# Four loads per pair in place of ten: one transfer for a graph's distances, one for its places and weights

## The chip, the cores and the metric

The kernel runs on one core of a Trainium2 chip. The metric is the device time of one execution in microseconds, the median of several runs. Times of single instructions come from one further execution, recorded by the hardware profiler.

## The reference

The input is 128 graphs of 64 nodes, with features `x` of 128 numbers per node and an adjacency `adj` whose entries serve as distances and as weights. Four layers follow each other, each as `x = layernorm(x + layer(x, adj))`. The first two are continuous-filter layers: every edge's distance is expanded in Gaussians and run through a small network; the result, weighted, multiplies the neighbour's features and is summed.

```python
# layer 0 (20 Gaussians); layer 1 is alike with 64 Gaussians, and adj squared as the weight
f_ij = exp(-0.5 / widths**2 * (d_ij - offsets)**2)
rcut = 0.5 * (cos(d_ij * pi / 5) + 1) * (d_ij < 5)
W = (ssp(f_ij @ fw1 + fb1) @ fw2 + fb2) * rcut       # ssp = softplus - log 2
agg = einsum('bjf,bijf->bif', x @ w_in2f, W)
out = ssp(agg @ ow1 + ob1) @ ow2 + ob2
```

Layers 2 and 3 are graph convolutions with a normalised adjacency.

## The kernel before

Most entries of `adj` are zero, so the kernel gathers the edges of each graph into a row of *slots*: for each slot the distance `d` (float32), the place `j` of the neighbour (bfloat16) and the weight `w` (float32). Two graphs make a pair, each on 64 of the 128 partitions; there are 64 pairs in each of the first two layers, in eight sets of eight pairs. The slots per graph (`GSLOTS`) depend on the set: 948 to 1092 in layer 0, 1140 to 1260 in layer 1. The gathering is done on the chip, set by set, beside the work on earlier sets: POOL scatters rows into DRAM (L1030), SP loads them back (`permuted`, L1052), DVE finds the edges (`nearest`, L1179 and L1182), POOL packs them (`pack`, L1097 to L1128), and SP stores the packed slots to DRAM (`store`, L1106), with one DRAM tensor for each of d, j and w of a set.

For each pair, `later_loads` (L1285) brings the slots back, repeated over partitions. In layer 0, 20 Gaussians fill 20 partitions, so the slots of a graph are cut into three chunks, laid one below the other: chunk 0 on partitions 0 to 19 of the graph's half, chunk 1 on 20 to 39, chunk 2 on 40 to 63. Each is a load of its own, so a pair has six loads of d. In layer 1, 64 Gaussians fill the 64 partitions and a graph's d is one load. j and w are each one load per graph, repeated over all 64 partitions. So a pair has ten loads in layer 0 and six in layer 1. All are issued by SP, except the first pair's d, which ACT issues (L1876).

The main loop (L1916) runs over 128 pairs times three chunks. At chunk 0 of pair n it issues the d loads of pair n+2, at chunk 1 those of j and w (`late`). The buffers: three of d, two each of j and w.

```python
def gaussians(n, step):          # d of pair n+1, at chunks 0 and 1 of pair n
    act(d, d, AF.Square, scale=-1.0, bias=w["off"])   # step 0
    act(d, d, AF.Exp, scale=w["coeff"])               # step 1
```

On ACT, `gaussians` turns d into Gaussians in place. On DVE, `one_hot` (L1762) compares j with the partition's number and multiplies by w, at chunk 0 of pair n. Then, chunk by chunk: PE multiplies by the first filter matrix (`px`, L1774), ACT takes Exp and Ln (`h`), PE multiplies by the second (`pw`, L1788), PE picks the neighbours' features through the one-hot (`pg`, L1800), ACT copies them (`g`), DVE multiplies the two (`m`, L1814) and sums slots (`agg`, L1837, L1841). ACT's instructions are recorded at the helper's line L951. The first matrix `fw1` has three versions, one per chunk, with the 20 rows of weights at that chunk's partitions and zeros elsewhere; so `px` takes all 64 partitions of a graph and only one chunk counts.

Within the main loop the program order of every engine, SP included, is the order in which the code is written (`in_order`, L1987); before it, only that of DVE and POOL is (L1914).

Of the kernel before, what the change touches and what calls it, by code (L numbers as in the profile page):

```python
# [12 lines left out]
F32 = mybir.dt.float32  # L13
AF = mybir.ActivationFunctionType
# [5 lines left out]
P = 128  # L20
A = 64
# [3 lines left out]
NG0 = 20  # L25
# [6 lines left out]
BF16 = mybir.dt.bfloat16  # L32
I32 = mybir.dt.int32
U32 = mybir.dt.uint32
U16 = mybir.dt.uint16
# [30 lines left out]
GSLOTS = tuple(tuple(4 * (a + b) for a, b in zip(*both)) for both in zip(EVEN, ODD))  # L66
CHUNKS = tuple(tuple(n // 3 for n in sizes) for sizes in GSLOTS)
MAX_SLOTS, MAX_CHUNK = max(map(max, GSLOTS)), max(map(max, CHUNKS))
# [533 lines left out]
def sparse_stack(ctx: ExitStack, tc: tile.TileContext, t: dict, out: bass.AP, flag):  # L602
# [11 lines left out]
    nc = tc.nc  # L614
# [9 lines left out]
    NS = NP // 8  # L624

    const = ctx.enter_context(tc.tile_pool(name="sconst", bufs=1))
    dram = ctx.enter_context(tc.tile_pool(name="sscratch", bufs=1, space=DRAM))
    edge = ctx.enter_context(tc.tile_pool(name="sedge", bufs=2))
    ps_n = ctx.enter_context(tc.tile_pool(name="sps_n", bufs=2, space=PSUM))

    def pair_at(n):

        return n // NP, (n + 8 * (n // NP)) % NP
# [87 lines left out]
    first = nc.cur_bb.bb.instructions[-1]  # L721

    def dram_ap(ap, offset, dims):
        return bass.AP(tensor=ap.tensor, offset=ap.offset + offset, ap=dims)
# [38 lines left out]
    neg_off = [const.tile([P, 1], F32, name=f"neg_off{i}") for i in range(2)]  # L763
    coeff0 = const.tile([P, 1], F32, name="coeff0")
    width0 = const.tile([P, 1], F32, name="width0")

    fw1 = const.tile([P, 3, C], F32, name="fw1")
# [2 lines left out]
    nc.vector.memset(width0, 1.0)  # L770
    for b in range(2):
        for k in range(3):
            at = slice(A * b + NG0 * k, A * b + NG0 * (k + 1))
            nc.scalar.dma_start(fw1[at, k, :], t["L0_gnn_fw1"])
        at = slice(A * b, A * b + 3 * NG0)
        for to, name in ((width0, "L0_gnn_widths"), (neg_off[0], "L0_gnn_offsets")):
            nc.scalar.dma_start(to[at, :], dram_ap(t[name], 0, [[0, 3], [1, NG0], [1, 1]]))

# [21 lines left out]
    def wait_steps(n):  # L802
        yield from (None for _ in range(n))
# [73 lines left out]
    with (  # L877
# [31 lines left out]
        to = const.tile([NB, 1], U32, name="graph_to")  # L909
# [30 lines left out]
    def act(out_, in_, func, **kw):  # L940
        nonlocal fence, latest, kind
        now = func == AF.Sin
        if kind is None or now != kind:
            fence = latest
            if not now:
                ctx_ = tc.issue_after(fence.ins) if fence is not None else nullcontext()
                with ctx_:
                    fence = nc.scalar.preload_act_table_set("natural_log_exp_and_others")
            kind = now
        with tc.issue_after(fence.ins) if fence is not None else nullcontext():  # L950
            latest = nc.scalar.activation(out_, in_, func, **kw)  # L951
        return latest
# [41 lines left out]
    def find_rows():  # L994
# [17 lines left out]
    perm_again = [dram.tile([P, A + 1], F32, name=f"perm_again{p}") for p in range(16)]  # L1012
    rows1 = [dram.tile([16 * A, 2, 40], F32, name=f"rows{s}") for s in range(NS)]
    slots = {
        (layer, name): [dram.tile([16, GSLOTS[layer][s]], dt, name=f"{name}{layer}_dram{s}") for s in range(NS)]
        for layer in range(2)
        for name, dt in (("d", F32), ("j", BF16), ("w", F32))
    }
    stored = set()

# [59 lines left out]
    def pack(layer, s, d, j):  # L1080

        caps, bases = CAPS[layer][s], BASES[layer][s]
        even, odds = EVEN[layer][s], ODD[layer][s]

        def packed(name, dt):
            tile_ = cpt.tile([P, max(EVEN[layer])], dt, tag=f"{name}{layer}", name=f"{name}{layer}_{s}")
            return tile_[:, 0:even]  # L1090

        dc, jc = packed("dc", F32), packed("jc", BF16)
        for r in range(8):
            to = slice(bases[r], bases[r] + caps[r])
            engine = nc.vector if layer + s == 0 and r % 2 else nc.gpsimd
            if layer == 0:
                engine.tensor_scalar(dc[:, to], d[:, r, 0 : caps[r]], -CUTOFF, None, ALU.max)  # L1097
            else:
                engine.tensor_copy(dc[:, to], d[:, r, 0 : caps[r]])
            if r % 2:  # L1100
                yield

        def store(name, tile_):
            for h, size in enumerate((even, odds)):
                to = dram_ap(slots[layer, name][s], h * even, [[even + odds, 64], [1, size]])
                nc.sync.dma_start(to, tile_[64 * h : 64 * (h + 1), 0:size])  # L1106

        store("d", dc)
        for r in range(8):
            to = slice(bases[r], bases[r] + caps[r])  # L1110
            nc.gpsimd.tensor_copy(jc[:, to], j[:, r, 0 : caps[r]])
        store("j", jc)
        w = packed("w", F32)
        if layer == 0:
            def sine():
                act(w, dc, AF.Sin, bias=half_pi, scale=PI / (2 * CUTOFF))

            if s == 0:
                sine()
            else:  # L1120
                yield from wait_steps(6)
                sines.append(sine)
                while sines:
                    yield
            yield from wait_steps(PACE if s else 0)
            (nc.gpsimd if s else nc.vector).tensor_tensor(w, w, w, ALU.mult)
        else:
            nc.gpsimd.tensor_tensor(w, dc, dc, ALU.mult)  # L1128
        store("w", w)
        stored.add((layer, s))  # L1130
        yield
# [148 lines left out]
    def loads(n, engine=nc.sync):  # L1280
        yield_, late = later_loads(n, engine)
        late()
        return yield_

    def later_loads(n, engine=nc.sync):  # L1285


        layer, p = pair_at(n)
        s = p // 8
        size = GSLOTS[layer][s]  # L1290
        at = (p % 8) * 2 * size
        assert (layer, s) in stored, "slots are read before they are written"
        d = edge.tile([P, MAX_SLOTS], F32, tag="d", name=f"d_{n}", bufs=3)
        j = edge.tile([P, MAX_SLOTS], BF16, tag="j", name=f"j_{n}")
        w = edge.tile([P, MAX_SLOTS], F32, tag="w", name=f"w_{n}")

        def load(to, name, first, n):

            (engine if name == "d" else nc.sync).dma_start(to, dram_ap(slots[layer, name][s], first, [[0, to.shape[0]], [1, n]]))  # L1299

        third = size // 3
        d = d[:, 0 : size if layer else third]
        for b in range(2):
            rows, first = slice(A * b, A * (b + 1)), at + b * size
            if layer == 1:
                load(d[rows], "d", first, size)
            else:
                for k, end in enumerate((NG0, 2 * NG0, A)):
                    load(d[A * b + NG0 * k : A * b + end], "d", first + k * third, third)

        def late():
            for b in range(2):
                rows, first = slice(A * b, A * (b + 1)), at + b * size
                load(j[rows, 0:size], "j", first, size)
                load(w[rows, 0:size], "w", first, size)

        return (d, j, w), late


    def load_a(s):  # L1320
# [142 lines left out]
    w = layers[0]  # L1463
    g0 = const.tile([P, 1], F32, name="g0")
    nc.vector.memset(g0, 0.0)
    act(g0[0:32], g0[0:32], AF.Square, bias=neg_off[0][0:32])
    act(g0[0:32], g0[0:32], AF.Exp, scale=coeff0[0:32])
    u = ps_n.tile([P, 512], F32, tag="n", name="zero_x")
    nc.tensor.matmul(u[:, 0:1], lhsT=fw1[0:32, 0, :], rhs=g0[0:32], start=True, stop=True)
    h0 = const.tile([P, 1], F32, name="h0")  # L1470
    act(h0, u[:, 0:1], AF.Exp, bias=w["b1"])
    act(h0, h0, AF.Ln, scale=0.5, bias=half)
    u = ps_n.tile([P, 512], F32, tag="n", name="zero_w")
# [442 lines left out]
    for i in range(3 * N + 2):  # L1916
        n, k = divmod(i, 3)
# [20 lines left out]
        if n < N:  # L1938
            layer, p = pair_at(n)
            q = next(q for q, group in enumerate(GROUPS[layer]) if group.start <= p < group.stop)  # L1940
            c = dict(
                id=f"{n}_{k}", n=n, k=k, s=p - GROUPS[layer][q].start, at=(layer, q), w=layers[layer],
                size=CHUNKS[layer][p // 8],
            )
            if k == 0:
                if n + GS < N:
                    ahead(n)
                if n + 2 < N:
                    slot_data[n + 2], late = later_loads(n + 2)
                if c["s"] == min(2, len(range(NP)[GROUPS[layer][q]]) - 1):  # L1950
                    load_nodes(layer, q)
                if n > 0:
                    one_hot(n)
                if layer == 1 and c["s"] == 0 and q in last:
                    last[q].append(normals_of(q))
            if k == 1 and n + 2 < N:
                late()
            filter_in(c)
# [76 lines left out]
```

## Time and profile before

| | |
|---|---|
| median of 3 runs | 1591.17 us (1591.0 to 1591.64) |
| the profiled execution | 1607.39 us, span of its instructions 1605.5 us |
| busy in the span | PE 89%, DVE 84%, ACT 83%, POOL 46% |
| start, before the first edges | 0 to about 75 us |
| layer 0's edges | about 75 to 745 us |
| layer 1's edges, with layers 2 and 3 of finished groups | about 745 to 1530 us |
| DMA | 205.67 MB in 122,289 packets |
| largest groups of work: PE pw, DVE m, PE pg | L1788, L1814, L1800 |

The views used below are the table of busy time in windows, the list of the instructions of one source line with those who waited for them, and the timeline, in which a bracket gives the idle time of the engine before an instruction and what ended it. "SPq" and "ACTq" are instructions of an engine's sequencer, such as the issue of a transfer; the number after the start is then the time that issuing took. Where "x6" ends a line of the timeline, six instructions in a row are merged.

### The profile page before, as it was taken

How to read it: one execution, taken by the hardware profiler on the slowest of the kernel's cores; microseconds unless marked ns; L12 is line 12 of the kernel's file. 1: busy time of each engine (PE TensorE's matmuls, PEld its weight loads, DVE VectorE, ACT ScalarE, POOL GpSimd, SP SyncE). 2: the span in 40 equal slices, each digit the busy share in tenths (PEclk: the TensorE clock that was granted, in tenths of full speed). 3: DMA queues.
4: the chain of work that ended last, by engine and by line, in shares of the span. 5: the costliest groups of instructions: out<-in, count | busy, mean ns of one | idle time of the engine just before them, and what ended most of it. 6: DMA issues, size and time to landing. Idle time of an engine off the chain costs nothing.

```text
span 1605.5 us, 24221 instructions
## 1 busy us (share of the span) xinstructions
PE 1432.6 (89%) x6813; PEld 802.6 (50%) x6813; DVE 1355.6 (84%) x3547; ACT 1335.6 (83%) x1847; POOL 732.5 (46%) x1174
## 2 busy tenths in 40 slices
PE   1276999999999999999999999999999999999974
PEld 1133454555554555555445555556555555555543
DVE  7687889999989999889878888888888888888873
ACT  1266898989888989889999998999989999899842
POOL 2425246555655644425611255433554435543454
PEclk9998999999999999999999999999999999999976
DMA  7654464645455544447555455544554455455200
GB/s 257 209 123 114 112 138 123 135 124 145 124 136 134 136 122 113 113 111 178 149 151 129 128 142 132 129 124 125 144 132 120 120 134 138 124 141 123 64 8 23
DMA packets 122289, 205.67 MB, mean 128 GB/s; under 512 B 47956, under 2 KB 80034, under 8 KB 121506
## 3 DMA queue, kind: packets, MB, share of 16 engines
q1 hardware_dynamic: 110784, 187.61, 46.7%
q0 software_dynamic: 6576, 14.99, 2.9%
q10 hardware_dynamic: 4786, 1.43, 0.4%
q8 instruction: 57, 0.93, 0.3%
q14 instruction: 86, 0.70, 0.2%
HBM read 185.29 MB, written 18.64 MB: 127 GB/s over the span
## 4 chain that ended last, share of the span: by engine, by line
PE 45%; DVE 27%; ACT 10%; DMA 7%; issue 6%; SPq 3%; POOL 2%; another core or an unknown queue 1%; ACTq 0%; DVEq 0%; POOLq 0%
PE pw L1788 16%; PE px L1774 9%; DVE m L1814 8%; PE pg L1800 7%; DVE agg L1837 6%; ACT h L951 4%; DVE hot L1762 2%; DVE at L1182 2%; PE hw L1673 2%; SPq L1299 2%; ACT g L951 2%; PE y L1453 2%; ACT d L951 1%; DVE st L1415 1%; PE o L1584 1%
## 5 line engine op out<-in xcount | busy, mean ns | idle before, releaser
L951 ACT ACTIVATE h<-h,half 128x672 f32<-128x672 f32 (+13 forms) x385 | 353.1, 917 | 0.1
L1837 DVE TENSOR_REDUCE agg<-m 128x16 f32<-128x240 f32 (+13 forms) x896 | 325.0, 411 | 3.0
L951 ACT ACTIVATE g<-pg 128x672 f32<-128x672 f32 (+12 forms) x384 | 303.2, 790 | 26.4 <-DVE m L1814 13.2
L1800 PE MATMUL pg<-hot,ys 64*128 64x336 f32 (+12 forms) x1536 | 308.8, 478 | 7.9 <-DVE hot L1762 7.0
L1788 PE MATMUL pw<-h,w_L_gnn_W2T 128*128 128x420 f32 (+5 forms) x768 | 301.9, 516 | 15.2 <-DVE m L1814 15.2
L1814 DVE SCALAR_TENSOR_TENSOR m<-pw,c_L_gnn_b,g 128x840 f32<-128x840 f32 (+5 forms) x192 | 200.9, 1046 | 115.6 <-PE pw L1788 88.0
L1788 PE MATMUL pw<-h,w_L_gnn_fw 128*128 128x336 f32 (+6 forms) x768 | 264.4, 467 | 28.3 <-DVE m L1814 22.0
L951 ACT ACTIVATE h<-px,c_L_gnn_b 128x840 f32<-128x840 f32 (+5 forms) x192 | 178.7, 931 | 53.6 <-PE px L1774 52.8
L1814 DVE SCALAR_TENSOR_TENSOR m<-pw,c_L_gnn_fb,g 128x672 f32<-128x672 f32 (+6 forms) x192 | 176.9, 921 | 50.0 <-PE pw L1788 31.2
L951 ACT ACTIVATE h<-px,c_L_gnn_fb 128x672 f32<-128x672 f32 (+6 forms) x192 | 159.3, 830 | 71.2 <-PE px L1774 46.4
L1788 PEld LDWEIGHTS pw<-h,w_L_gnn_W2T 128*128 128x128 f32 x768 | 132.5, 191 | 141.1 <-DVE m L1814 37.6
L1774 PE MATMUL px<-d,fw 64*128 64x336 f32 (+6 forms) x768 | 166.2, 507 | 40.8 <-DMA d<-d_dram 29.2
L1800 PEld LDWEIGHTS pg<-hot,ys 64*128 64x128 f32 x1536 | 146.3, 188 | 108.1 <-issue 17.5
L1788 PEld LDWEIGHTS pw<-h,w_L_gnn_fw 128*128 128x128 f32 x768 | 132.5, 191 | 120.6 <-DVE m L1814 62.2
L1762 DVE SCALAR_TENSOR_TENSOR hot<-j,row,w 128x1212 f32<-128x1212 bf16 (+12 forms) x128 | 177.0, 1383 | 9.0 <-issue 9.0
L1774 PE MATMUL px<-d,w1t 64*128 64x420 f32 (+5 forms) x768 | 181.1, 548 | 1.7 <-ACT h L951 1.6
L1422 POOL TENSOR_SCALAR rs<-mv 128x4 f32<-128x4 f32 x61 | 14.5, 237 | 344.0 <-DVE mv L1416 335.6
L1774 PEld LDWEIGHTS px<-d,fw 64*128 64x128 f32 x768 | 59.7, 188 | 132.2 <-ACT h L951 44.4
L951 ACT ACTIVATE d<-d,neg_off 128x1212 f32<-128x1212 f32 (+12 forms) x128 | 119.8, 936 | 7.1 <-issue 7.1
L1428 POOL TENSOR_SCALAR x_all<-ny,mv,rs 128x128 f32<-128x128 f32 x124 | 116.4, 947 | 3.3
L1030 POOL DMA_INDIRECT rows<-comb,goes x64 | 67.9, 1061 | 97.1 <-DMA rows<-comb,goes 69.6
L1774 PEld LDWEIGHTS px<-d,w1t 64*128 64x128 f32 x768 | 57.8, 184 | 66.8 <-ACT g L951 26.8
(264 smaller groups left out, 2209.6 us busy)
## 6 DMA issues: line engine op xcount, KB each, us to landing
d<-d_dram SPq DMA_DIRECT2D x32, 315.0 KB
w<-w_dram SPq DMA_DIRECT2D x32, 315.0 KB
d<-d_dram SPq DMA_DIRECT2D x32, 303.0 KB
w<-w_dram SPq DMA_DIRECT2D x32, 303.0 KB
w<-w_dram SPq DMA_DIRECT2D x32, 252.0 KB
j<-j_dram SPq DMA_DIRECT2D x32, 157.5 KB
j<-j_dram SPq DMA_DIRECT2D x32, 151.5 KB
d<-d_dram SPq DMA_DIRECT2D x16, 300.0 KB
```

The source lines that it names most:

```text
L951: latest = nc.scalar.activation(out_, in_, func, **kw)
L1030: nc.gpsimd.indirect_dma_start(out=into, out_offset=bass.IndirectOffsetOnAxis(ap=at, axis=0), in_=rows, in_offset=None,)
L1182: nc.vector.max_index(out=at[:, r, cut], in_max=top[:, r, cut], in_values=av[:, r, :])
L1299: (engine if name == "d" else nc.sync).dma_start(to, dram_ap(slots[layer, name][s], first, [[0, to.shape[0]], [1, n]]))
L1428: (nc.gpsimd if n == GS else nc.vector).tensor_scalar(dst[:, s, :], y[:, s, :], mv[:, s, 0:1], rstd[:, s : s + 1], ALU.subtract, ALU.mult,)
L1453: nc.tensor.matmul(ps[:, s, :], lhsT=xt[:, s * P : (s + 1) * P], rhs=w["win"], start=True, stop=True)
L1762: nc.vector.scalar_tensor_tensor(hots[n][:, 0:size], j[:, 0:size], near, wt[:, 0:size], ALU.is_equal, ALU.mult)
L1774: nc.tensor.matmul(ps[:, b, 0:n], lhsT=w1, rhs=d[rows, col : col + n], start=True, stop=True)
L1788: nc.tensor.matmul(c["pw"][:, b, :], lhsT=c["w"]["w2"], rhs=c["h"][:, b, :], start=True, stop=True)
L1800: nc.tensor.matmul(ps[:, b, 0:n], lhsT=y[rows, :], rhs=hots[c["n"]][rows, at], start=True, stop=True,)
L1814: nc.vector.scalar_tensor_tensor(messages[n][:, :, at], c["pw"], c["w"]["b2"], c["g"], ALU.add, ALU.mult)
L1837: nc.vector.tensor_reduce(av[:, :, :, r], both, AX.X, ALU.add)
```

## The change

The distances. The 60 partitions that hold Gaussians are numbered differently: partition 3g + k of a graph's half now has Gaussian g of chunk k. So one transfer with a source of 20 repeats by three chunks writes 60 partitions in turn. The last four partitions of each half are no longer loaded; three fixed buffers `distances` replace the pool's three of d, and are set to zero once by POOL at the start. The matrix `fw1`, the widths and the offsets follow the new numbering.

Places and weights. The stores of j and w of a set go to one DRAM tensor of 16-bit words, a graph's w (two words a slot) followed by its j. One load per graph brings both into one tile, of which j and w are views.

A pair then has two loads of d and two of `jw`, in both layers. When they are issued, and how many buffers there are, stays. A small matmul before the main loop takes 64 rows in place of 32.

```diff
-            at = slice(A * b + NG0 * k, A * b + NG0 * (k + 1))
+            at = slice(A * b + k, A * b + 3 * NG0, 3)
             nc.scalar.dma_start(fw1[at, k, :], t["L0_gnn_fw1"])
...
-            nc.scalar.dma_start(to[at, :], dram_ap(t[name], 0, [[0, 3], [1, NG0], [1, 1]]))
+            nc.scalar.dma_start(to[at, :], dram_ap(t[name], 0, [[1, NG0], [0, 3], [1, 1]]))
+    distances = [const.tile([P, MAX_SLOTS], F32, name=f"distances{i}") for i in range(3)]
+    for d in distances:
+        nc.gpsimd.memset(d[:, 0 : max(CHUNKS[0])], 0.0)
...
         def store(name, tile_):
+            both = even + odds
             for h, size in enumerate((even, odds)):
-                to = dram_ap(slots[layer, name][s], h * even, [[even + odds, 64], [1, size]])
-                nc.sync.dma_start(to, tile_[64 * h : 64 * (h + 1), 0:size])
+                from_ = tile_[64 * h : 64 * (h + 1), 0:size]
+                if name == "d":
+                    to = dram_ap(slots[layer, "d"][s], h * even, [[both, 64], [1, size]])
+                else:
+                    wide = 2 if name == "w" else 1
+                    to = dram_ap(
+                        slots[layer, "jw"][s], wide * h * even + 8 * both * (name == "j"),
+                        [[12 * both, 16], [wide * both, 4], [1, wide * size]],
+                    )
+                    from_ = from_.bitcast(U16)
+                nc.sync.dma_start(to, from_)
...
-        d = edge.tile([P, MAX_SLOTS], F32, tag="d", name=f"d_{n}", bufs=3)
-        j = edge.tile([P, MAX_SLOTS], BF16, tag="j", name=f"j_{n}")
-        w = edge.tile([P, MAX_SLOTS], F32, tag="w", name=f"w_{n}")
...
+        jw = edge.tile([P, 3 * MAX_SLOTS], U16, tag="jw", name=f"jw_{n}")[:, 0 : 3 * size]
         third = size // 3
-        d = d[:, 0 : size if layer else third]
+        d = distances[n % 3][:, 0 : size if layer else third]
         for b in range(2):
-            rows, first = slice(A * b, A * (b + 1)), at + b * size
+            first = at + b * size
             if layer == 1:
-                load(d[rows], "d", first, size)
+                to, dims = d[A * b : A * (b + 1)], [[0, A], [1, size]]
             else:
-                for k, end in enumerate((NG0, 2 * NG0, A)):
-                    load(d[A * b + NG0 * k : A * b + end], "d", first + k * third, third)
+                to, dims = d[A * b : A * b + 3 * NG0], [[0, NG0], [third, 3], [1, third]]
+            engine.dma_start(to, dram_ap(slots[layer, "d"][s], first, dims))
...
             for b in range(2):
-                rows, first = slice(A * b, A * (b + 1)), at + b * size
-                load(j[rows, 0:size], "j", first, size)
-                load(w[rows, 0:size], "w", first, size)
+                from_ = dram_ap(slots[layer, "jw"][s], 3 * (at + b * size), [[0, A], [1, 3 * size]])
+                nc.sync.dma_start(jw[A * b : A * (b + 1), :], from_)
```

## The prediction

> **What bounds the kernel now.** I read the table of windows first, cut at the first matmul on edges (about 76 us) and at the change of layer (about 745 us). Its columns are the stretch, its length, the busy time of PE, weight loads, DVE, ACT and POOL, the granted clock, the DMA share and GB/s.
>
> ```profile
> 67.00:76.00 9.00, 0.75 (x2) 0.57 (x4) 0.14 (x1) 1.19 (x2) 7.01 (x8) 1.00 0.63 175
> 76.00:160.00 84.00, 61.84 (x257) 30.62 (x255) 62.23 (x220) 54.73 (x76) 33.85 (x46) 0.92 0.51 123
> 160.00:640.00 480.00, 452.06 (x2170) 245.17 (x2168) 451.51 (x1397) 422.97 (x628) 242.94 (x407) 1.00 0.52 129
> 745.00:1500.00 755.00, 734.61 (x3499) 410.36 (x3498) 629.66 (x1317) 703.22 (x883) 339.24 (x398) 1.00 0.53 134
> ```
>
> In the body of layer 0 (160 to 640) PE and DVE are both busy 94% of the time and ACT 88%; in layer 1 PE is busy 97%. The DMA engines are half used. So the body is bound by PE with DVE and ACT close behind, and the changed loads matter only where one of these waits for a load, or where SP, which issues them, holds something up. Only the stretches before 160 have real idle time.
>
> Second, the view of the load line, L1299: who waited for its transfers over the whole run.
>
> ```profile
> L1299 SPq DMA_DIRECT2D d<-d_dram x506: 3/329/1575, 68.9 to 1488.1; - x169
> L1299 SPq DMA_DIRECT2D j<-j_dram x256: 444/587/2004, 66.3 to 1495.0; - x128
> L1299 SPq DMA_DIRECT2D w<-w_dram x256: 444/595/1756, 69.8 to 1495.6; - x128
> L1299 ACTq DMA_DIRECT2D d<-d_dram x6: 279/336/471, 67.6 to 70.2; - x6
> ...
>   PE px L1774: 29.2, 1
>   DVE hot L1762: 9.0, 1
>   POOL rows L1030: 7.1, 3
>   ACT d L951: 7.1, 1
> ```
>
> Each wait of PE, DVE and ACT occurs once, and all three are the first pair. In 127 of 128 pairs no computing engine waited for a load. Third, the timeline of ACT and SP around that first pair.
>
> ```profile
> 67.58 2.93 ACTq L1299 DMA_DIRECT2D d<-d_dram  x6
> 73.97 0.59 ACT L951 ACTIVATE d<-d,neg_off 128x360 f32<-128x360 f32 x1 [7.06 <-issue]
> 74.60 0.59 ACT L951 ACTIVATE d<-d,coeff 128x360 f32<-128x360 f32 x1
> ...
> 69.75 2.39 SPq L1299 DMA_DIRECT2D w<-w_dram  x2
> 72.18 1.67 SPq L1299 DMA_DIRECT2D d<-d_dram  x4
> ```
>
> The six loads of the first pair's distances are issued one after another until 70.51; Square starts at 73.97, Exp ends at 75.19 and the first px is at 75.25. This chain sets when the edge pipeline starts. The one-hot of this pair (DVE, 76.16 to 77.50) needs j and w; its user pg starts at 79.20, so it has 1.7 us of slack.
>
> **What the Trainium skill says.** "DMA: Bandwidth & Descriptors", section "Rules for kernel authors", tells to coalesce small transfers, since under 64 KB one pays mostly overhead; the loads removed are 24.7 to 34.1 KB. But its section "Issuing engines are not separate DMA queues" says that where a transfer is issued changes only the sequencer's time. The row that decides between a real gain and a hidden one is the list of waiters above: the overhead sits on SP and is waited for once. The forecast goes by the row. The same page ("Why a DMA increments its semaphore by 16 and not by 1") says that a transfer is spread over the largest number of DMA engines up to 16 that divides the slowest dimension of both its sides. By it, 20 rows use 10 engines and 24 rows 12; the new load, 60 rows against a source whose slowest dimension is 20, uses 10. Six rows on each of ten engines before, six after: an estimate from that page that the landing time doesn't change. No view of this trace shows single DMA engines.
>
> **The change part by part.**
>
> *SP's issue, layer 0.* Removed per pair: six d at 0.33 us and four j or w at 0.59 us, with about 0.05 us between them: 6 x 0.38 + 4 x 0.64 = 4.8 us of SP. Added: two d and two jw. A load of 64 rows takes 0.59 whatever its length (j and w, half as long, agree), so 4 x 0.64 = 2.6 us. SP gains 2.2 us per pair, 64 x 2.2 = 141 us. Nothing of it is on the path: the waits of PE, DVE and ACT on loads past the first pair are zero. The cover is the lead: d of pair n+2 is issued in pair n and first read in pair n+1, a pair later, 669/64 = 10.5 us. Cover gone would show as ACT waiting at Square.
>
> *SP's issue, layer 1.* Two fewer, 1.3 us per pair. From 745 to 1500 SP waits 247.0 us on the one-hot and 188.8 us on px, for buffers to come free; SP has time to spare. Zero.
>
> *The bytes.* d loads 60 rows of 64, 6% less of d; j and w keep their bytes in half as many packets. With the share at 0.52, zero; both ends within 1 us.
>
> *Semaphores.* Square waits for two loads in place of six, one_hot for two in place of four. DVE has 252 separate semaphore instructions at one_hot (median 49 ns), 2 x 128 x 49 ns = 12.5 us at most if they were exposed. But 212.01 (hot) follows 211.72 + 0.37 (agg) with the usual overlap, so they run under the preceding instruction. Taken as zero, bound: 0 to 12 us gained. I see no way to a loss.
>
> *Start of layer 0.* Two d on ACT's queue in place of six: 2 x 0.64 = 1.3 against 2.93 us, the last issue ends at 68.9 in place of 70.5. Square keeps its distance of 3.46 us from it: 72.3, a gain of 1.7 us. The next limit is one_hot: jw can only be issued when w's store has landed (69.75, as w now). Two issues in place of the stretch 69.75 to 72.14 with its slow w; so one_hot keeps its time or gains a little, and its slack of 1.7 us just covers the shift. Value 1.7, bounds 0 (j or w decides) and 2.5. It carries through: DVE waits 7.39 us for the first pw behind its in-order side work, so everything later moves along.
>
> *POOL and the constants.* Three memsets of 128x364 on POOL; the near row is the 128x384 memset of fw1, 0.41 us, so 1.2 us, in the first 3 us. They delay tie (2.29), read by DVE at 2.80, which is then idle 1.99 us for the first entries; and POOL later idles 17.8 us before L911. Zero. Strided loads of fw1 have the same 20 rows; 64 rows in the zero matmul in place of 32: nothing. The stores keep count and rows; no engine but POOL waits on them.
>
> Sum: 1.7 us against the profiled run of 1607.39 (span 1605.5, 1.9 around it). The three unprofiled times have a median of 1591.17, 16.2 less; a start-up saving carries over whole: 1591.2 - 1.7 = **1589.5**. About 0.2% (3.2 us) is what a measurement of this kernel can tell from no change, so this lies inside.
>
> **Rivals.**
>
> *Faster: the stalls without a name go.* In the crowded opening all engines stop twice with their inputs ready:
>
> ```profile
> 147.46 1.16 PE L1534 MATMUL zs<-zt,ys 128*128 128x128 f32 x8 [2.00 <-issue]
> 153.54 2.77 PE L1788 MATMUL pw<-h,w_L_gnn_fw 128*128 128x360 f32 x4 [4.92 <-issue]
> ...
> 158.09 0.86 ACT L951 ACTIVATE h<-px,c_L_gnn_fb 128x720 f32<-128x720 f32 x1 [10.68 <-remote]
> ```
>
> The px it needs began at 143.98. The other is at 100.67 (2.86 us). Both stand where DMA share is 0.75 to 0.95 (0.93 at 142 to 144), with SP issuing without pause. With fewer packets they may shrink: 3 to 13 us, 1578 to 1587. Against it: the bytes stay, and the unprofiled runs, 16 us shorter, may not have these stalls.
>
> *Slower: the same stall falls elsewhere.* SP issues in shorter time, so its loads, the permuted rows and POOL's scatters bunch more tightly between 76 and 200. Place: ACT and DVE at the first chunk of a pair; price 2.9 to 10.7 us each time; it decides from one extra stall of 5 us on, as 1.7 is gained: about 1597. For it: the stall exists and its cause isn't in the view. A far worse, unlikely form of a late load is d landing over one pair late (were its 86 KB on one engine, at 220 to 300 GB/s over 16 engines, some 17 GB/s each, 5 us a graph, 10 a pair): then ACT would wait in each of 64 pairs.
>
> *SP's relief reaches the computing engines.* Packing and gathering of later sets run off SP and POOL; if DVE waited for them, up to some 10 us of layer 0's 6% idle PE would go: 1582. Against: DVE's waits there name PE and ACT, never POOL or DMA.
>
> *It does less than it says.* The start is set by j and w: 1591.2, no change.
>
> **How the numbers follow.** Forecast 0.43 (0.37 within 0.2%, 0.06 faster), stalls gone 0.23 (mostly faster), relief reaches 0.07 (faster), stall elsewhere or late loads 0.20 (0.19 slower), nothing 0.07 (same). Faster 0.35, same 0.45, slower 0.20. The range takes most of the first rival and half of the slower: 1580 to 1598; the forecast's own range is 1588.5 to 1591.5.
>
> **What would show it.** Right: L1299 has 4 loads per pair, SP's waits in layer 0 grow by some 140 us, Square of the first pair starts near 72.3, the first px near 73.5, and PE's busy time in the body is unchanged. Wrong: a computing engine waiting on d or jw after the first pair, a shorter pair time in the body, or a change of the stalls at 100 and 147.

## The result: slower by 0.4%

The changed kernel takes 1598.74 us (median of 10 runs, 1596.4 to 1602.95), the kernel before, beside it on the same chip, 1591.69 us (10 runs). The ratio is 1.0040, with a 95% interval of 1.0028 to 1.0051: some 6 to 7 us more. Forecast was 1589.5 us.

The profiled execution of the changed kernel spans 1600.0 us, that of the kernel before 1605.5. These two spans can't be compared: the one of before holds a stall of about 12.7 us at 147 to 158 us and one of 2.9 us at 100 us, put down to "remote", which none of the other fourteen traces has. Without them it would be some 1590.

**Windows of the changed kernel** (stretch, its length, busy time of PE, weight loads, DVE, ACT and POOL, granted clock, DMA share, GB/s):

```profile
67.00:78.20 11.20, 0.04 (x2) 0.07 (x2) 3.74 (x28) 4.17 (x5) 8.20 (x19) 1.00 0.26 71
78.20:160.00 81.80, 66.39 (x275) 32.36 (x275) 64.67 (x230) 59.17 (x82) 34.53 (x47) 0.98 0.56 131
160.00:640.00 480.00, 452.75 (x2182) 246.65 (x2182) 455.89 (x1404) 423.78 (x630) 254.20 (x426) 1.00 0.55 129
745.00:1500.00 755.00, 733.12 (x3486) 409.49 (x3482) 626.13 (x1302) 700.74 (x880) 345.75 (x404) 1.00 0.55 132
```

PE's busy time in the body is what it was (452.75 against 452.06 of 480 us). The bound has not moved, and fewer loads have not loosened it.

**The two load lines**, d (L1317) and places with weights (L1322): count, then the least, median and greatest time of an issue in ns, then who waited for what they bring (us, times).

```profile
L1317 SPq DMA_DIRECT2D distances<-d_dram x254: 444/754/1466, 73.2 to 1483.6; - x127
L1317 ACTq DMA_DIRECT2D distances<-d_dram x2: 747/768/789, 73.2 to 74.0; - x2
...
  ACT distances L954: 4.3, 1
```

```profile
L1322 SPq DMA_DIRECT2D jw<-jw_dram x256: 444/545/1107, 76.6 to 1489.9; - x128
...
  DVE hot L1769: 11.4, 1
```

There are four loads per pair, and each wait still occurs once, in the first pair. Packets went from 122,289 to 98,504. SP's waits between 160 and 640 us went from 102.6 to 244.1 us: the relief is real, and stays on SP.

**The timeline of ACT, SP and DVE at the first pair:**

```profile
69.50 1.28 ACT L954 ACT_TABLE_LOAD   x1 [17.11 <-DVE dc L1102]
73.21 1.58 ACTq L1317 DMA_DIRECT2D distances<-d_dram  x2
73.22 3.30 SPq L1317 DMA_DIRECT2D distances<-d_dram  x4
76.64 2.42 SPq L1322 DMA_DIRECT2D jw<-jw_dram  x4
76.84 0.59 ACT L954 ACTIVATE distances<-distances,neg_off 128x360 f32<-128x360 f32 x1 [4.34 <-DMA distances<-d_dram]
...
84.12 1.34 DVE L1769 SCALAR_TENSOR_TENSOR hot<-jw,row 128x1080 f32<-128x1080 bf16 x1 [11.39 <-DMA jw<-jw_dram]
```

Of the kernel before, the same table load and the same one-hot:

```profile
63.91 1.28 ACT L951 ACT_TABLE_LOAD   x1 [17.24 <-DVE dc L1097]
...
76.16 1.34 DVE L1762 SCALAR_TENSOR_TENSOR hot<-j,row,w 128x1080 f32<-128x1080 bf16 x1 [9.03 <-issue]
```

The table load, with which ACT begins the last steps ahead of the first pair, stands at 69.50; before it stood at 63.91. Square starts at 76.84 and not at 72.3 as forecast. From the table load on, Square comes 7.34 us later (before 10.06), which is a gain, but the one-hot comes 14.62 us later (before 12.25), which is a loss. So the first question is where 5.6 us went ahead of all edges.

**What stands ahead.** In the list of who waited for whom, SP's queue between 20 and 31 us; first the kernel before, then the changed one.

```profile
SPq L891 <- DMA neg_off<-in_neg_offsets_dram: 13.3, 1, 13.3
SPq L1323 <- DMA fw<-in_L_gnn_fw_dram: 3.3, 1, 3.3
```

```profile
SPq L894 <- DMA neg_off<-in_neg_offsets_dram: 14.1, 1, 14.1
SPq L1330 <- DMA fw<-in_L_gnn_fw_dram: 5.0, 1, 5.0
```

SP waits for loads that ACT issued, though it doesn't read what they bring: the loads on both queues share a set of completion semaphores, and the next user of one waits for the last. SP's load of `a_all` (L1323, after: L1330) waits in this way for the fifth of the six loads of `fw1` (L774), which has the same semaphore. That load is issued at 22.38 us before and at 25.48 after; the semaphore's last update comes at 26.19 and 29.48, and `a_all` is issued 0.02 us later at most. The six became slower to issue when their target became every third partition. Their lines before and after:

```profile
L774 ACTq DMA_DIRECT2D fw<-in_L_gnn_fw_dram x6: 287/332/606, 14.5 to 23.0; - x6
```

```profile
L774 ACTq DMA_DIRECT2D fw<-in_L_gnn_fw_dram x6: 736/737/774, 15.5 to 26.3; - x6
```

So the load of `a_all` is issued at 29.50 in place of 26.20. POOL's scatter of the whole adjacency (2 MB, `adj_sorted`) is issued at 26.87 before and 27.07 after: the load was just ahead of it, and is now behind. The scatter's packets move from 29.37 to 36.56 before and from 29.92 to 37.19 after; the load has landed at 29.49 before, and at 39.07 after. What that costs is seen at `permuted`, PE's first use of `a_all`, before and after:

```profile
33.34 3.65 PE L1060 MATMUL permuted<-a_all,there 128*128 128x64 f32 x16 [0.15 <-PE sorted L975]
```

```profile
39.21 3.01 PE L1065 MATMUL permuted<-a_all,there 128*128 128x64 f32 x13 [5.81 <-DMA a_all<-in_adj_dram]
```

Issue 3.3 us later, work 5.9 us later.

### The profile page after: what moved, and what is told of

Its sections match the earlier page's. It is cut to its first block, busy times and chain, and to the rows that moved or that the text cites. A ratio compares the mean times of both kernels' runs of the same rounds, so it can differ in the third digit from the quotient of the medians.

```text
span 1600.0 us, 23482 instructions
## 1 busy us (share of the span) xinstructions
PE 1432.1 (90%) x6813; PEld 802.1 (50%) x6813; DVE 1356.3 (85%) x3547; ACT 1336.0 (83%) x1847; POOL 739.5 (46%) x1177
## 4 chain that ended last, share of the span: by engine, by line
PE 44%; DVE 26%; ACT 11%; DMA 7%; issue 6%; POOL 5%; SPq 0%; ACTq 0%; DVEq 0%; POOLq 0%
PE pw L1795 16%; PE px L1781 9%; DVE m L1821 7%; PE pg L1807 7%; DVE agg L1844 5%; ACT h L954 5%; DVE hot L1769 2%; DMA out_dram<-gz,at_row 2%; POOL x_all L1435 2%; ACT g L954 2%; DVE at L1197 2%; PE hw L1680 2%; ACT distances L954 1%; PE y L1460 1%; DVE st L1422 1%
## 5 line engine op out<-in xcount | busy, mean ns | idle before, releaser
L1781 PE MATMUL px<-distances,fw 64*128 64x336 f32 (+6 forms) x768 | 165.5, 508 | 34.0 <-ACT distances L954 26.4
L1769 DVE SCALAR_TENSOR_TENSOR hot<-jw,row 128x1212 f32<-128x1212 bf16 (+12 forms) x128 | 176.6, 1379 | 11.4 <-DMA jw<-jw_dram 11.4
L1781 PE MATMUL px<-distances,w1t 64*128 64x420 f32 (+5 forms) x768 | 181.1, 548 | 1.7 <-ACT h L954 1.6
L1429 POOL TENSOR_SCALAR rs<-mv 128x4 f32<-128x4 f32 x61 | 15.1, 248 | 329.4 <-DVE mv L1423 321.6
L954 ACT ACTIVATE distances<-distances,neg_off 128x1212 f32<-128x1212 f32 (+12 forms) x128 | 119.9, 936 | 4.3 <-DMA distances<-d_dram 4.3
L1781 PEld LDWEIGHTS px<-distances,fw 64*128 64x128 f32 x768 | 59.0, 188 | 125.5 <-issue 60.6
L1035 POOL DMA_INDIRECT rows<-comb,goes x64 | 68.6, 1072 | 107.6 <-DMA rows<-comb,goes 88.0
L1781 PEld LDWEIGHTS px<-distances,w1t 64*128 64x128 f32 x768 | 57.8, 184 | 66.8 <-ACT g L954 26.8
```

What stands on the lines that cost most here:

```text
L1035: nc.gpsimd.indirect_dma_start(out=into, out_offset=bass.IndirectOffsetOnAxis(ap=at, axis=0), in_=rows, in_offset=None,)
L1769: nc.vector.scalar_tensor_tensor(hots[n][:, 0:size], j[:, 0:size], near, wt[:, 0:size], ALU.is_equal, ALU.mult)
L1781: nc.tensor.matmul(ps[:, b, 0:n], lhsT=w1, rhs=d[rows, col : col + n], start=True, stop=True)
```

## Experiments

Thirteen more kernels; the ratio is to the kernel before on the same chip, and medians in us of different chips can't be compared. To compare stages I took the starts of PE's `px`, three chunks to a pair; chunks are counted from 1. "Rest of layer 0" ends, and "layer 1" begins, at the `px` of chunk 192, the last of layer 0; layer 1 ends at that of the last chunk, 384. In us:

| kernel | first `px` | first six pairs | rest of layer 0 | layer 1 | ratio, 95% interval |
|---|---|---|---|---|---|
| before | 75.25 | 68.7 | 597.5, stalls in it | 785.2 | 1 |
| after | 78.16 | 72.2 | 583.5 | 788.3 | 1.0040 (1.0028 to 1.0051) |
| b_fw1 | 80.36 | 68.0 | 582.0 | 785.4 | 1.0016 (1.0004 to 1.0028) |
| jw_alone | 74.72 | 68.1 | 582.7 | 785.6 | 1.0011 (0.9997 to 1.0025) |
| d_alone | 79.75 | 68.4 | 581.1 | 785.6 | 1.0019 (1.0008 to 1.0029) |
| a_early | 74.95 | 70.8 | 582.7 | 787.7 | 1.0008 (0.9992 to 1.0024) |
| b_early | 74.76 | 67.3 | 580.9 | 785.2 | 0.9985 (0.9969 to 1.0) |
| b_fw1_early | 76.12 | 68.6 | 580.8 | 785.2 | 0.9989 (0.9978 to 1.0) |
| a_jw_act | 76.87 | 72.4 | 582.9 | 786.3 | 1.0015 (1.0004 to 1.0025) |
| a_split0 | 73.28 | 69.1 | 581.5 | 786.5 | 1.0008 (0.9992 to 1.0023) |
| a_early_pe | 74.52 | 70.7 | 582.3 | 787.4 | 1.0013 (1.0003 to 1.0023) |
| a_split0_pe | 75.77 | 70.6 | 582.0 | 787.1 | 1.0015 (1.0004 to 1.0026) |
| jw_pe | 77.61 | 68.1 | 580.9 | 787.3 | 1.0019 (1.0004 to 1.0033) |
| a_early_pe32 | 74.33 | 73.6 | 583.3 | 786.6 | 1.0002 (0.9992 to 1.0012) |
| a_split0_pe32 | 75.68 | 72.1 | 581.3 | 786.8 | 1.0004 (0.9989 to 1.0020) |

Each stage time is of one execution, and layer 0's scatter by a microsecond or two. Layer 1 is steadier. The executions of one kernel themselves spread over some 6 us, so a stage time says where something moved, and the ratio says what it is worth.

### Which part loses: parts alone

**b_fw1**, the strided `fw1` alone:

```diff
-            at = slice(A * b + NG0 * k, A * b + NG0 * (k + 1))
+            at = slice(A * b + k, A * b + 3 * NG0, 3)
...
-            nc.scalar.dma_start(to[at, :], dram_ap(t[name], 0, [[0, 3], [1, NG0], [1, 1]]))
+            nc.scalar.dma_start(to[at, :], dram_ap(t[name], 0, [[1, NG0], [0, 3], [1, 1]]))
```

> The kernel before with only the new numbering of fw1, widths and offsets (their six loads write every third partition); the distances keep their six loads and their old places, so the first layer's filter output is not the reference's. Theory 1 (start): the strided loads take 0.74 us each to issue in place of 0.33, hold back the first adjacency load by some 3 us until it stands behind POOL's 2 MB scatter, and everything after it comes 5.5 to 6 us later: about 1597. Theory 2 (the big loads slow the body; the late start was chance): no change, 1591.

Measured 1596.58 us, ratio 1.0016 (1.0004 to 1.0028). Its timeline at the start:

```profile
27.12 1.91 POOL L911 DMA_INDIRECT adj_sorted<-entries,graph_to  x1 [18.05 <-DVE graph_to L910]
...
29.05 0.39 SPq L1323 DMA_DIRECT2D a_all<-in_adj_dram  x1
...
38.63 1.73 PE L1060 MATMUL permuted<-a_all,there 128*128 128x64 f32 x7 [5.19 <-DMA a_all<-in_adj_dram]
```

An edit that adds no work makes the whole delay of the start: load at 29.05, behind the scatter, `permuted` at 38.63, first `px` at 80.36, the latest of all kernels, since it lacks the shorter d loads. In time it costs less than the 5.1 us by which that `px` is later: the ratio comes to 2.5 us (0.6 to 4.5), where 5.5 to 6 were expected. Theory 2, no change, is ruled out; the size isn't settled by this run.

**jw_alone** has the kernel before with places and weights in one load (the stores and loads of `jw` from the diff, all of d as before), **d_alone** the opposite (`distances`, its loads, `fw1`).

> The kernel after with the distances loaded as before (six loads, old numbering); only places and weights are merged. Theory 1: fw1's loads are not strided, so the start is as before but for the first pair's jw coming up to 2 us late: 1591 to 1593. Theory 2: the large jw loads are what costs, so the whole loss stays: about 1598.

> The kernel before with only the distances merged (new numbering, fixed buffers); j and w stay four loads. Theory 1: the late start of 5.6 us is there, and the first pair's distances come some 2.7 us sooner of it, but the one-hot decides: 1594 to 1597. Theory 2: no large loads, so 1591 or less.

Measured 1594.13 us, 1.0011 (0.9997 to 1.0025), for jw_alone and 1596.99, 1.0019 (1.0008 to 1.0029), for d_alone. jw_alone issues `a_all` at 26.66 and has `permuted` at 33.13; d_alone issues it at 29.34 and has `permuted` at 40.53, after a wait of 7.19 us. The body tells against the other theory: the rest of layer 0 takes 581.1 to 582.7 us with ten, eight or six loads per pair, and layer 1 785.4 to 785.6. The loads of one part alone give nothing and cost nothing there. The ratios of the two parts add up to 1.0030, against 1.0040 for both together; the intervals are too wide to tell these apart.

### Mending the start

**a_early**, the changed kernel with the first load of `a_all` moved ahead of those of x:

```diff
+        a_first = adj.rearrange("(p b) i j -> (b i) p j", b=2)[:, 0:8, :]
+        nc.sync.dma_start(a_all[:, 0:8, 0:A], a_first)
         for into, at in x_parts:
...
-    load_a(0)
```

> The kernel after with one load moved: SP brings the first eight pairs' adjacency right after the entries, ahead of x, not behind the loads whose semaphores it waits for. Theory 1: the 5.8 us wait of the permuting matmul for this load goes, and the time falls by 5 to 6 us against the kernel after: about 1593. Theory 2: as after, 1598 to 1599.

Measured 1594.15 us, 1.0008 (0.9992 to 1.0024). The intervals of a_early and of the changed kernel don't meet: moving one load gives back 1.0040 - 1.0008 = 0.0032, some 5 us. Its start:

```profile
10.21 0.39 SPq L894 DMA_DIRECT2D a_all<-in_adj_dram  x1
...
33.55 3.65 PE L1067 MATMUL permuted<-a_all,there 128*128 128x64 f32 x16
```

Square then stands at 73.64 and the first `px` at 74.95. The expected 1593 was about reached. Not all is mended: the table load is at 65.91, 2.0 us later than before.

The same move in the kernel before (**b_early**) and in b_fw1 (**b_fw1_early**) tells whether the strided loads act in this way alone.

> The kernel before with the first set's load of a_all moved ahead of the loads of x at the start, nothing else. Theory 1 (the loss lies in the start, where the a_all load is issued late and lands late): before issued it at 26.2 us, POOL's scatter of 2 MB begins at 27, and permuted ran at 33.34 us with almost no wait for it, so there is nothing or little to gain in a typical execution: 0 to 1.5 us less than before, 1590 to 1592 us; permuted starts between 32.5 and 33.6. Rival (a load ahead of x delays the first entries, DVE's index work starts later): 1 to 3 us more than before, with permuted at 34.5 or later.

> The kernel before with the strided loads of fw1 (and the order of widths and offsets that goes with them), as in b_fw1, and the load of a_all moved ahead. Output of layer 0 is not the reference's, since fw1's rows lie elsewhere. Theory 1 (strided fw1 loads cost only by way of the late a_all load): the same as b_early within 1.5 us, permuted at about 33.5, the sine table load at about 64. Rival (the strided loads also delay something else of the start, as the table load at 65.9 in a_early hints): 2 us more than b_early, the sine table load 2 us later than in b_early.

Measured 1590.98 us, 0.9985 (0.9969 to 1.0), and 1592.32, 0.9989 (0.9978 to 1.0). With the load early, the strided `fw1` costs nothing that the times show: 1.0016 became 0.9989, and the intervals of b_fw1 and b_fw1_early don't meet. The rival was right in a detail, for the table load is 1.9 us later (65.54 against 63.64). This is a second way in which slow `fw1` loads reach the start: ACT issues small weights behind them, and its copy of the permuted rows, which comes right after the last of these issues, starts at 40.98 in place of 37.94. b_early is the fastest kernel here, though its interval ends at 1.

How near the edge the load stands is shown by a kernel made for another purpose, jw_pe (below). There it is issued behind the scatter, and still isn't late:

```profile
27.43 1.91 POOL L915 DMA_INDIRECT adj_sorted<-entries,graph_to  x1 [18.34 <-DMA c_L_gnn_b<-in_L_gnn_b_dram]
27.86 0.39 SPq L1332 DMA_DIRECT2D a_all<-in_adj_dram  x1
...
33.91 1.30 PE L1066 MATMUL permuted<-a_all,there 128*128 128x64 f32 x5
```

The scatter takes 1.91 us to issue, and its packets move only from 31.63 on; the load has landed at 31.22. So 0.43 us behind the start of the scatter's issue did no harm, and 1.93 us (b_fw1) to 2.43 us (after) made `permuted` wait 5.2 to 7.2 us. No run stands in between.

### The late first one-hot

In a_early the one-hot still starts 14.67 us after the table load (12.25 before). Neither part alone makes it so late: 13.02 in jw_alone, 12.04 in d_alone. SP now issues four d loads in 3.3 us before any of `jw`. **a_jw_act** lets ACT issue the first two `jw` loads; **a_split0** loads the places of the first pair apart and early, as before, with its weights on ACT's queue.

```diff
-                nc.sync.dma_start(jw[A * b : A * (b + 1), :], from_)
+                engine.dma_start(jw[A * b : A * (b + 1), :], from_)
```

```diff
+            if n == 0:
+                for cut, queue in ((slice(2 * size, 3 * size), nc.sync), (slice(0, 2 * size), engine)):
+                    for b in range(2):
...
+                        queue.dma_start(jw[A * b : A * (b + 1), cut], from_)
+                return
```

> The changed kernel with the early a_all load (a_early), and the first pair's two jw loads issued by ACT right after its two d loads, in place of SP, which issues them after four d loads of 3.3 us. Theory (the first one-hot is late because SP issues the jw loads last): one_hot of the first pair starts 1.5 to 3 us sooner after the sine table load than in a_early (14.67 us), the time falls by as much: 1591.5 to 1593. Rival (the jw loads land late because they are long, 2 x 64 rows of 6 KB, and share the DMA engines with the d loads): one_hot starts within 0.7 us of a_early's distance, no change of the time (1594).

> The changed kernel with the early a_all load (a_early); in the first pair alone the places are loaded by themselves on SP as soon as they are stored, and the weights by ACT's queue after the d loads; all other pairs keep four loads. Theory (start only): one_hot of the first pair starts at most 12.3 us after the sine table load (14.67 in a_early, 12.25 before), the time falls by 2 to 3 us against a_early: 1591 to 1592, the same as before, and the rest of layer 0 and layer 1 take what they take in the kernel before (582 to 583, 785.5 us). Rival (jw loads cost something in layer 1, whose stretch took 788 us in both the changed kernel and a_early): 1593.5 to 1595, with layer 1 at 788 again.

Measured 1595.37 us, 1.0015 (1.0004 to 1.0025), and 1594.66, 1.0008 (0.9992 to 1.0023). In a_jw_act:

```profile
71.75 1.46 ACTq L1324 DMA_DIRECT2D jw<-jw_dram  x2
75.55 0.59 ACT L956 ACTIVATE distances<-distances,neg_off 128x360 f32<-128x360 f32 x1 [6.62 <-DMA distances<-d_dram]
...
81.17 1.34 DVE L1770 SCALAR_TENSOR_TENSOR hot<-jw,row 128x1080 f32<-128x1080 bf16 x1 [12.01 <-DMA jw<-jw_dram]
```

The loads were issued from 71.75 on and not from 73.11, yet one_hot starts 15.25 us after the table load (65.92), no sooner, and Square is 1.9 us later. My theory of the issue order fell, and the rival's forecast held: within 0.7 us, and no gain. That the loads in flight slow each other fits both shifts. The windows from the issue of the first pair's last kind of load to its one-hot, of the kernel before (from the first load of w) and of a_early (from the first of `jw`), fit as well:

```profile
69.75:76.16 6.41, 0.91 (x4) 0.57 (x4) 0.00 (x0) 1.19 (x2) 4.88 (x6) 1.00 0.76 203
```

```profile
73.11:80.58 7.47, 3.23 (x8) 1.13 (x8) 0.00 (x1) 4.29 (x6) 5.61 (x6) 1.00 0.94 230
```

The DMA share is 0.94 in place of 0.76. Before, the places, 135 KB a graph, had been issued at 66.28 and 68.19 already, when little else moved; now they are the end of a load of 405 KB that can't be issued before w is stored. But a_split0, which gives them back their early load, had the one-hot 12.74 us after the table load, nearly as before, and its two variants below 14.31 and 14.30: one lucky trace, no cure, and none in the times. No run took the other loads out of the way, so what makes the first jw late stays open.

### Layer 1: a refill of instructions

After and a_early took 788.3 and 787.7 us in layer 1, each part alone 785.6. The difference sits in two chunks, 343 and 355, where PE waits for `x_all`, which POOL makes late, since its scatter of `out_dram` waits for the last one to land. In the view of DMA queues, q8 carries 16 KB packets of instructions, one per 26 us or so; in a_early one stands 14.9 and one 14.3 us before the two px, while a scatter is under way. The Trainium skill ("Runtime: NRT & Kernel Launch", section "Instruction fetch mechanics") says that an engine's instructions are refilled in blocks of 16 KiB, 256 instructions. The trace agrees for PE: jw_alone has some 14,100 recorded instructions of PE and 57 such packets, 248 to a packet, and some records can be missing.

So whoever changes PE's stream moves the fetches, and the change did. PE's `px` waits for the loads of d, and for these waits it has separate semaphore instructions in its stream. Their count, before and after:

```profile
L1774 PEldq EVENT_SEMAPHORE  x257: 51/51/51, 71.5 to 1515.6; - x129
```

```profile
L1781 PEldq EVENT_SEMAPHORE  x129: 51/51/2157, 75.9 to 1511.1; - x129
```

With two loads of d for six in layer 0, two go in each of the 64 pairs: 128 in all, half a period of 256. (In jw_alone there are 257, in d_alone 129.) In layer 1 the fetches of the changed kernel therefore stand elsewhere. That alone doesn't cost: in d_alone they stand 16.3 and 13.9 us before the px of chunks 343 and 355, and neither is late.

One-column matmuls at the start, where PE is idle, move them too:

```diff
+        fill = ps_pre.tile([1, 1], F32, name="fill")
+        for _ in range(64):
+            nc.tensor.matmul(fill, lhsT=ident[:, 0:1], rhs=ident[:, 0:1], start=True, stop=True)
```

**a_early_pe** and **a_split0_pe** have 64 of them, **jw_pe** is jw_alone with 89.

> The changed kernel with the early a_all load (a_early), and 64 one-column matmuls on PE in the first microseconds, where PE waits for nothing yet: they only push PE's later instructions back in its stream by 128 places (64 weight loads and 64 matmuls). Theory (in layer 1 a refill of PE's instructions, a 16 KB packet of queue q8, falls in the same microsecond as a scatter of out_dram and sends the next scatter behind the long jw loads; it stood 14.8 and 14.4 us before the px of chunks 343 and 355 in the changed kernel): the refill moves some 13 us, POOL's wait for out_dram goes from 26.4 us back to 21 to 22, layer 1 takes 785.4 in place of 787.7 us, the time falls by 1 to 2.5 us against a_early. Rival (the long jw loads alone delay the scatters, or the fixed distances buffers do): layer 1 at 787 to 788 and POOL's wait at 26 as before.

> a_split0 with the same 64 one-column matmuls. Here only one of the two places was delayed (chunk 343, layer 1 took 786.5 us). Theory of the refill: layer 1 785.4 us, POOL's wait for out_dram 21 to 22 in place of 24.3 us; with all three losses gone the time is that of the kernel before within 1.5 us. Rival (loads of four per pair cost something that no trace showed): 2 us or more above the kernel before, as a_split0 (1594.7 against 1592.0).

> The kernel before with only places and weights in one load (jw_alone), and 89 one-column matmuls on PE at the start, 178 places in its stream: in jw_alone 178 recorded PE instructions lie between the point 14.8 us before the px of chunk 343 and the refill that fell 4 us after it, so the refill should now fall on the spot of the changed kernel. Theory of the refill: the scatter of out_dram there lands 4 us later, POOL's wait for out_dram rises from 21.7 to 24 or more, layer 1 from 785.6 to 786.5 to 788. If the refill misses the spot by more than a microsecond it tells nothing. Rival: refill on the spot and layer 1 still at 785.6, the wait still at 21.7.

Measured 1595.71, 1595.67 and 1595.57 us. The first two tell nothing of the theory, and it was my mistake: a float32 matmul is recorded as two weight loads and two matmuls, so 64 are 256 places, one whole period. One more packet (57 for 56), no fetch moved, layer 1 at 787.4 and 787.1. jw_pe got 356 places, one period and 100. It missed chunk 343, the spot aimed at, so by its own terms the expectation isn't tested there. But a fetch fell 14.7 us before the px of chunk 331. POOL's timeline there in jw_alone and in jw_pe, with what it waited for in brackets:

```profile
1274.45 1.96 POOL L1635 TENSOR_TENSOR blocks<-a_all,dinv 64x256 f32<-64x256 f32 x3 [1.31 <-DMA out_dram<-gz,at_row]
1276.69 1.00 POOL L1032 DMA_INDIRECT out_dram<-gz,at_row  x1 [0.28 <-POOL blocks L1635]
1279.26 0.96 POOL L1032 DMA_INDIRECT out_dram<-gz,at_row  x1 [1.57 <-DMA out_dram<-gz,at_row]
```

```profile
1276.64 1.96 POOL L1639 TENSOR_TENSOR blocks<-a_all,dinv 64x256 f32<-64x256 f32 x3 [2.25 <-DMA out_dram<-gz,at_row]
1278.88 2.08 POOL L1036 DMA_INDIRECT out_dram<-gz,at_row  x1 [0.28 <-POOL blocks L1639]
1285.22 0.96 POOL L1036 DMA_INDIRECT out_dram<-gz,at_row  x1 [4.26 <-DMA out_dram<-gz,at_row]
```

The scatter under way lands a microsecond later; the next takes 2.08 us to issue in place of 1.00, and is still under way when SP issues two jw loads (1280.11; in jw_alone 1278.85, as it lands), so POOL waits 4.26 us for it. Chunk 331 took 5.21 us in place of 3.87, and layer 1 787.3 in place of 785.6. The delay of the changed kernel was made in a kernel that had none there. In time the two can't be told apart (1.0019 against 1.0011).

The opposite, with 32 matmuls, half a period:

> a_early with 32 one-column matmuls at the start. In float32 each is two passes, so two weight loads and two matmuls: a_early_pe's 64 put 256 places into PE's stream, just one refill period, and moved nothing (fetches 14.9 and 14.4 us before the px of chunks 343 and 355 as before, one fetch more at 5.27 us); 32 put 128 places in, half a period of 26.5 us. Theory of the refill: no fetch between 20 and 13.5 us before the px of chunks 331, 343 and 355, the scatters there land 9 us before it and not 5 to 6, POOL's wait for out_dram is 21 to 22.5 us in place of 26.4, layer 1 takes 785.5 to 786 in place of 787.7 us; the time falls by 1 to 2.5 us against a_early and a_early_pe (1594.2, 1595.7). Rival (loads of four per pair delay the scatters wherever the refill is): layer 1 at 787 to 788 and the wait at 26 again.

> a_split0 with 32 one-column matmuls at the start: the changed kernel with all three found losses mended (late a_all, late first jw, refill on the scatter). Theory: layer 1 785.5 to 786 us, the time 1 to 2 us below a_split0_pe and within 1.5 us of the kernel before. Rival (something else of the changed loads costs time that the stages do not show): 2 us or more above the kernel before with an interval that leaves out 1.

Measured 1594.9 us, 1.0002 (0.9992 to 1.0012), and 1594.91, 1.0004 (0.9989 to 1.0020), the kernel before beside them 1593.88. The 128 places put the fetches of a_early_pe32 back where the kernel before has them: 7.67 us before the px of chunk 331 (before: 7.56), 0.49 behind that of chunk 343 (0.51). Chunks 343 and 355 take 3.84 us each, in place of 4.96 and 5.17. POOL at chunk 343:

```profile
1329.44 1.95 POOL L1642 TENSOR_TENSOR blocks<-a_all,dinv 64x256 f32<-64x256 f32 x3 [1.06 <-DMA out_dram<-gz,at_row]
...
1334.53 0.96 POOL L1041 DMA_INDIRECT out_dram<-gz,at_row  x1 [1.85 <-DMA out_dram<-gz,at_row]
```

But layer 1 took 786.6 us, not 785.5 to 786, and POOL's wait is 24.1 us: a fetch now stands 15.1 us (a_split0_pe32: 15.3) before the px of chunk 283, and that chunk is late (4.54 and 5.07 us against 3.98 in a_early). The delay moves with the refill. The times don't show the gain: 1.0002 and 1.0008 (a_early) have intervals that overlap.

Such scatters come every twelve chunks, for chunks 247 to 379. Over all fifteen traces, 14 of these chunks are late, by 0.5 to 1.4 us. Twelve of them have a fetch 14.3 to 15.3 us before their px, and of all such fetches one alone does no harm (jw_alone, 15.3 us before chunk 283). None of eleven fetches 13.7 to 14.2 us before does any. The other two late chunks have a fetch 17.2 and 17.9 us before (chunk 331 in a_split0_pe and in the changed kernel), while four at 17.1 to 17.3 in other kernels do nothing. So the refill sets it off, and whether it grows depends on more than its time. Whether it needs the long jw loads isn't shown: in no kernel with j and w apart did a fetch fall 14.3 to 15.3 us before such a chunk.

## Why the prediction was wrong, step by step

**The step that failed** is "Strided loads of fw1 have the same 20 rows; 64 rows in the zero matmul in place of 32: nothing." I counted rows and bytes and not the time of an issue: 0.74 us each in place of 0.33. Nor did I look who waits behind them on the other queue. Six loads gave 2.6 us on ACT's queue (11.48 against 8.91). With 1.0 us by which they begin later (15.50 against 14.46), that is 3.3 us on SP's queue, and 5.9 at `permuted`, because a load of `a_all` lost its place ahead of a scatter of 2 MB. By after against a_early that is about 5 us of the loss of 6 to 7; b_fw1, which has this step alone, lost 2.5 (0.6 to 4.5), so the path is shown and its price only roughly. The trace of before held the warning: L1323 was issued at 26.20, 0.67 us ahead of the scatter, after a wait for "fw".

**The start's gain** was right in kind and mis-sized: 1.7 us forecast, from the issue alone with the landing kept at 3.46 us; the table load to Square became 2.7 us shorter. 1.3 of that is issue, and 1.4 landing, which the estimate from the Trainium skill ("DMA: Bandwidth & Descriptors", section "Why a DMA increments its semaphore by 16 and not by 1") had left unchanged. The issue of a merged d takes 0.75 us and not 0.59.

**One_hot's slack** failed as well. "One_hot keeps its time or gains a little" was wrong by 2.4 us (14.62 against 12.25), and pg waited 3.25 us for it. The first px gained from d what the first pg lost.

**The body of layer 0**: zero forecast, zero found. SP's waits rose by 141.5 us between 160 and 640 alone, where the forecast had some 140 for all of layer 0; its relief reached no computing engine. The Trainium skill's rule to coalesce what is under 64 KB ("DMA: Bandwidth & Descriptors", section "Rules for kernel authors") gave nothing here, as the row of waiters had said; of the loads removed, only those of d were that small (j and w have 135 and 270 KB in the first pair).

**Semaphores**: "I see no way to a loss" looked at the time of these instructions on ACT and DVE, and at PE's not at all. 128 fewer in PE's stream gained nothing that shows, and moved the refills; in the changed kernel these then fell on three scatters of layer 1 (chunks 331, 343 and 355), though not in d_alone.

**Rivals.** "The stalls go" can't be credited: they are missing in the traces with ten loads too. "Slower: the same stall falls elsewhere" named the right sign and the wrong place; what comes nearest is layer 1's delays, 2 to 3 us of the trace, by a cause I hadn't thought of. That the measured time lies near the 1597 of this rival is luck.

**What stays open**: why the first jw lands late, what besides its time makes a refill cost something, and how much of the loss is left with the early load. a_early against b_early is 1.0008 against 0.9985, with intervals that meet; the traces show 2.4 us at the one-hot and 2.5 in layer 1.

## What to carry to other kernels

Cost an edit to a constant's layout as you would one in the loop: look at the time its loads take to issue, and at everything that waits behind them on any queue, for two queues can be tied by completion semaphores that neither needs. A load that has to get ahead of a large scatter, and whose issue hangs on another queue, stands at a cliff: here some 3 us of delay made its reader 5 to 6 us late. Issue it early (a_early gave 5 us for one moved line). And merging transfers for which nobody waited bought nothing, though their number fell from ten to four.

## What the runs showed of the hardware

A load of 20 rows onto every third partition took 0.74 us to issue, onto 20 partitions in a row 0.33. A load of 256 KB issued 0.43 us behind the start of a 2 MB scatter's issue landed in 3.4 us, one issued 2.4 us behind it in 9.6. A refill of PE's instructions, one 16 KB packet per some 250 recorded instructions, went with a delay of 0.5 to 1.4 us in 14 chunks where it fell beside a scatter with long loads next; 356 places more in PE's stream made such a delay where there was none, and 128 took two away and made another. So in a trace, a difference of 1 or 2 us between two versions of such a kernel may belong to the refills and not to the edit, even if the edit does nothing but remove waits.
